# Soft-disc attention layer: paired norm-factor products, work moved from ScalarE to VectorE, and units of work in a new order

## The chip, the cores and the metric

The kernel runs on one core of a Trainium2 chip, in float32. The time is that of one execution in device microseconds (us). Engines go by the names of the profile: PE is TensorE's matmuls, PEld its weight loads, ACT is ScalarE, DVE is VectorE, POOL is GpSimd, SP is SyncE, which only issues transfers. Each engine works through its own list of instructions in the order in which the program gives them, and waits on semaphores where it needs another engine's result.

## The reference

The input is a batch of eight images of 32x32 tokens with 256 channels. Four layers follow one another, each `x = x + f(groupnorm(x))`. The change touches the last one, the soft-disc layer, whose `f` is, cut to what matters:

```python
qkv = silu(x @ w_qkv.T)
q, k, v = split(qkv, 3)                       # 8 heads of 32 channels
q = rope(rms_norm(q, w_qn)); k = rope(rms_norm(k, w_kn))   # norms per head
wp = silu(x @ w_wp.T + b_wp)                  # 16 columns: a width and a sharpness per head
width = sigmoid(wp[..., :8]) * max_dist + 0.5
sharp = sigmoid(wp[..., 8:]) * 9.5 + 0.5
scores = einsum(q, unfold(k)) / sqrt(32)      # 7x7 window around each token
soft_mask = sigmoid((width - rel_dist) * sharp)
attn = softmax(scores - (1 - soft_mask) * 10000)
out = einsum(attn, unfold(v))
return silu((rms_norm(out, w_on) + v) @ w_out.T)
```

The last norm runs over all 256 channels and has one weight per channel, `w_on`. The rope acts along the head axis's positions as the reference writes it; nothing of the change bears on it.

## The kernel before, in words

The kernel is a Python program that writes out the instructions of each engine. The soft-disc layer is `layer3` (L1950 on), with its attention in the class `DiscStream` (L1634 on).

**Tiling.** Channels lie on the 128 partitions, in two chunks of four heads; a chunk of an image is numbered J = 2b + c. Tokens are cut into 8 pairs of 8x8 blocks. A group is one pair of one chunk, so there are 8 x 2 x 8 = 128 groups, and the main loop takes one step n per group, 16 steps per image. Chunks are worked on well ahead of the step that uses them.

**A step** (the loop behind `start()`, at the end of `layer3`) writes, in this order: scores of n+3 on PE (16 matmuls of 32 rows, L1665); exponentials of n on ACT (`exps`, L1688, which also sum); the planned units due at n; logits of n+3 on DVE (L1678); the first half of `turn(n-2)`, PE transposes of the probabilities (`pt`, L1706) with a DVE copy to `pts` (L1711); `finish()`; `soft(n+5)`, the tanh of the disc on ACT (L2076); `divide(n)`, a DVE reciprocal (L1695) and a POOL product (L1696); the units due at n+0.5; the second half of the turn; `finish()`; `values(n-3)` on PE (`o`, L1722) with its DVE copies (L1730); and `masked(n+5)` on POOL (L2083). Probabilities live in a ring of nine tiles `e`.

**PSUM.** All PE outputs of the layer come from one ring of 8 banks (`st.ring(...)`), taken in the order written. A matmul into a bank waits until the last reader of the bank's earlier content is done.

**Units.** `Fillers` holds work with due times, in steps. `units(at)` emits what is due. A unit issues its PE part (and sometimes an ACT part) and may return a function, its rest; `finish()` calls all rests that are waiting. With n = 8J for a chunk and n = 16b for an image, the units and their due times are:

- `project(J, s, h)`: a projection of half an image (`qkv_ps`, L2015: PE, then a tanh on ACT, L2000; the rest on DVE, L2025/L2027, and for Q and K a POOL square, L2035). K at n-12 and n-11.5, Q at n-11 and n-10.5, V at n-7.5 and n-7.
- `roots(J, t)` at n-8: mean-square matmuls (`ms_ps`, L2095 for the heads, L2102 for the output norm of an earlier image) and, on ACT, a table load, Ln and Exp (L2109 to L2111) that give the factors `fac`; the next tanh loads the other table (L2076).
- `head_scale(J, s, h)`: one matmul of 32 rows that spreads a norm factor over the channels (`fac_ps`, L2117), and as its rest a DVE product with K or Q (L2121). At n-6, -5.5, -5 and -4.5.
- `in_strips` at n-6 copies values to padded strips on POOL; `vturn(J, u)`, five per chunk, transposes them on PE (`vt`, L1739) and copies them to `v` on ACT (L1744).
- `discs(b, u)` at n-10 and n-9.5: the width and sharpness (`wp_ps`, L2048), then in one rest a DVE add (L2055), an ACT tanh (L2060), a DVE product (L2061), an ACT tanh (L2062) and three small DVE operations from L2065.
- `normed(b, c)` at n-13.5 and n-13: the normalised input on ACT (L419).
- the tail of image b: `tail_sq` at n+19 and n+20 (POOL, L2145); four `tail_scale` at n+30, 30.5, 31, 31.5 (a 32-row matmul, L2150, DVE product L2154, POOL add L2155); `output` at n+33.5, 39, 39.5 and 41.5 (`out_ps`, L2163, an ACT tanh, a DVE product L2170, a POOL add L2172 and a store), with a `reload` three steps earlier.

In plain order of the engines' lists, units with the same due time stand in the order in which they were added. `First3.early` (L362 on) loads and prepares the constants, `won` and `spread` among them, long before the layer.

Of the kernel before, what the change touches and what calls it, by code (L numbers as in the profile page):

```python
# [32 lines left out]
def shape_constants():  # L33
    f = np.float32
    p = np.arange(P)
    k = {}

    k["k_id"] = np.stack(
        [np.eye(P), (p[:, None] // 8 == p[None] // 8) / 8.0], 1
    ).astype(f)  # L40


    same = (p[:, None] // 32 == p[None] // 32).astype(np.float64)
    k["k_hd"] = np.stack([np.eye(P) - same / 32, same / 32], 1).astype(f)
# [41 lines left out]
    one[:, 8] = 1.0  # L86
    k["k_sel3"] = np.concatenate(
        [(p[:, None] // 32 == np.arange(32)[None]) / 32.0, one / 256.0], 1
    ).astype(f)
    k["k_spread"] = (p[:, None] % 32 == p[None] // 32).astype(f)  # L90
    return {n: np.ascontiguousarray(v) for n, v in k.items()}


# [12 lines left out]
def layouts(inputs):  # L106
# [36 lines left out]
    a["l3_qkn"] = np.concatenate(  # L143
        [np.tile(i["L3_conv_w_" + n], 4) for n in ("qn", "kn")]
    )
    a["l3_on"] = i["L3_conv_w_on"].reshape(2, P)
    a.update(shape_constants())
    return {n: np.ascontiguousarray(v) for n, v in a.items()}

# [202 lines left out]
class First3(First):  # L352
# [8 lines left out]
    def early(self):  # L361
# [25 lines left out]
        def factors():  # L387
            won, spread = self.won, self.spread
            nc.vector.tensor_scalar(self.bwp, self.bwp, 0.5, None, ALU.mult)
            nc.gpsimd.tensor_scalar(self.wo, self.wo, 0.5, None, ALU.mult)  # L390
            nc.vector.tensor_mul(won[:, 0], won[:, 0], won[:, 1])
            nc.vector.scalar_tensor_tensor(
                spread[:, 0], won[:, 0], -(32.0**-0.5) / MASK_SCALE, spread[:, 0],
                ALU.mult, ALU.mult,
            )
            nc.vector.memset(won, 0.0)

        def weight():
            for h in range(2):
                nc.sync.dma_start(  # L400
                    self.won[32 * h + 8 : 32 * h + 9], a["l3_on"].unsqueeze(0)
                )

        return [loads, factors, weight]

# [1228 lines left out]
class DiscStream(Stream):  # L1634
# [7 lines left out]

    def __init__(self, K, wk, cp, pp, pairs, n_img, ebufs):
        super().__init__(K, wk, pp, pairs, n_img, ebufs)
        self.slots, self.s = 20, {}
        shape = [P, 4, 2 * self.PART]
        self.tiles = [cp.tile(shape, F32, name=f"e{i}") for i in range(ebufs)]

# [34 lines left out]

    def exps(self, n):
        mx, e = self.mx.pop(n), self.prob(n)
        self.su = self.wk.tile([P, 4], F32, name="su", bufs=4)
        for j in range(4):
            self.nc.scalar.activation(  # L1688
                e[:, j], e[:, j], AF.Exp, scale=-1.0, bias=mx[:, j : j + 1],
                accum_out=self.su[:, j : j + 1],  # L1690
            )

    def divide(self, n):
        e = self.prob(n)
        self.nc.vector.reciprocal(self.su, self.su)  # L1695
        self.nc.gpsimd.tensor_mul(e, e, self.su.unsqueeze(2).to_broadcast([P, 4, NWIN]))  # L1696

    def turn(self, n, i):

# [35 lines left out]
    def value_unit(self, strips, dst, u):  # L1735
        ps = self.ring("vt")
        for i in range(4):
# [3 lines left out]
                strips[:, col, 8 * r : 8 * r + 8].rearrange("p i j -> p (i j)"),  # L1741
                self.K.ident,
            )
        self.nc.scalar.copy(  # L1744
            dst[: self.PART, 4 * u : 4 * u + 4, :],
            ps[: self.PART, :].rearrange("p (s c) -> p s c", c=P),
        )
# [202 lines left out]
def layer3(tc, K, src, dst, n_img, a, first):  # L1950
    nc = tc.nc
    pairs = disc_pairs()
    with tc.tile_pool(name="l3c", bufs=1, reuse_waits="tile") as cp, tc.tile_pool(
# [14 lines left out]
        for i in range(3):  # L1968
            st.clear(i)
        K.ring = st.ring  # L1970
        bwp, sel, spread, won = first.bwp, first.sel, first.spread, first.won
        wo, win, eps = first.wo, first.win, first.eps

        gn = first.gn
# [66 lines left out]
        def discs(b, u):  # L2041
# [11 lines left out]
            def rest():  # L2053
# [2 lines left out]
                    d, ps.rearrange("p (t g) -> p t g", g=P)[:, :, 0:16],  # L2056
                    bwp.unsqueeze(1).to_broadcast([P, 4, 16]),
                )
                th = wk.tile([P, 4, 16], F32, name="dth")
                nc.scalar.activation(th, d, AF.Tanh)  # L2060
                nc.vector.scalar_tensor_tensor(d, th, 1.0, d, ALU.add, ALU.mult)  # L2061
                nc.scalar.activation(d, d, AF.Tanh, scale=0.5)  # L2062
                wd, sp = d[:, :, 0:8], d[:, :, 8:16]
                md = math.sqrt(2.0) * 3
                nc.vector.tensor_scalar(wd, wd, md / 2, md / 2 + 0.5, ALU.mult, ALU.add)  # L2065
# [45 lines left out]
            nc.scalar.activation(r[:n], r[:n], AF.Exp, scale=-0.5)  # L2111
            fac[J] = r

        def head_scale(J, s, h):
            g = slice(32 * (2 * s + h), 32 * (2 * s + h) + 32)
            ps = st.ring("fac_ps")
            nc.tensor.matmul(ps, spread[g, s], fac[J][g], start=True, stop=True)  # L2117

            def rest():
                d = dest(J, s, h)  # L2120
                nc.vector.tensor_mul(d, d, part(ps))  # L2121

            return rest

# [11 lines left out]
        def vturn(J, u):  # L2136
            b, c = divmod(J, 2)
            if u == 0:
                st.v[b, c] = wk.tile([P, st.slots, P], F32, name="v", bufs=2)
            st.value_unit(strips, st.v[b, c], u)  # L2140


        def tail_sq(b, c):
            sqs["o", c] = wk.tile([P, L], F32, name="sq", bufs=4)
            nc.gpsimd.tensor_mul(sqs["o", c], st.o[b, c], st.o[b, c])  # L2145

        def tail_scale(J, b, c, h):
            g, hs = slice(32 * h, 32 * h + 32), slice(h * HALF, (h + 1) * HALF)
            ps = st.ring("fac_ps")
            nc.tensor.matmul(ps, won[g, c], fac[J][g], start=True, stop=True)  # L2150

            def rest():
                d = st.o[b, c][:, hs]
                nc.vector.tensor_mul(d, d, ps)  # L2154
                nc.gpsimd.tensor_add(d, d, vT[b, c][:, hs])  # L2155

            return rest

# [26 lines left out]
        def plan_chunk(J):  # L2185
# [4 lines left out]
            for i in range(4):  # L2190
                s, h = 1 - i // 2, i % 2
                fill.add(n - 12 + i / 2, lambda s=s, h=h: project(J, s, h))
                fill.add(n - 6 + i / 2, lambda s=s, h=h: head_scale(J, s, h))
            fill.add(n - 7.5, lambda: project(J, 2, 0))
            fill.add(n - 7, lambda: project(J, 2, 1))
            fill.add(n - 6, lambda: in_strips(J))

        def plan_image(b):
            n = 16 * b
            if b:  # L2200
# [6 lines left out]
                fill.add(max(n - 21, -1), lambda: gn.mean(b, later))  # L2207
                fill.add(max(n - 19, 1), lambda: gn.root(b, later))
                for c in range(2):
                    fill.add(n - 13.5 + c / 2, lambda c=c: normed(b, c))  # L2210
                for u in range(2):
                    fill.add(n - 10 + u / 2, lambda u=u: discs(b, u))
            for c in range(2):
                fill.add(n + 19 + c, lambda c=c: tail_sq(b, c))
                for h in range(2):
                    fill.add(
                        n + 30 + c + h / 2,
                        lambda c=c, h=h: tail_scale(2 * b + 4, b, c, h),
                    )
            for i in range(4):  # L2220
                at = n + 32 + (1.5, 7, 7.5, 9.5)[i]
                fill.add(at - 3, lambda i=i: reload(b, i // 2, i % 2))
# [2 lines left out]
        for J in range(2 * n_img + 3):  # L2225
            b, c = divmod(J, 2)
            t = b - 2 if c == 0 and b >= 2 else None
            if J and (J < 2 * n_img or t is not None):
                fill.add(8 * J - 8, lambda J=J, t=t: roots(J, t))
            if J < 2 * n_img:  # L2230
                plan_chunk(J)
        for b in range(n_img):
            plan_image(b)
        for J in range(2 * n_img):
# [10 lines left out]
                    later.append(r)  # L2245

        def finish():
            while later:
                later.pop(0)()

        def start():

            units(-11)
            rest = [discs(0, 0), discs(0, 1), project(0, 1, 0)]
            rest[0]()
            rest[2]()
            r = project(0, 1, 1)
            rest[1]()
            r()
            soft(0)  # L2260
            for h in range(2):
                project(0, 0, h)()
# [4 lines left out]
            masked(0)  # L2267
            roots(0, None)
            in_strips(0)
            for i in range(4):  # L2270
                head_scale(0, 1 - i // 2, i % 2)()
            masked(1)
            for i in range(3, 9):
                st.clear(i)
# [4 lines left out]
        with tc.manual_schedule(engines={E.PE, E.Activation, E.DVE, E.Pool}):  # L2279
            start()  # L2280
            for n in range(-4, N + 3):
                if 0 <= n + 3 < N:
# [1 line left out]
                    if t is pairs[0]:  # L2284
                        st.o[b, c] = wk.tile([P, L], F32, name="oT", bufs=5)
                    st.scores(n + 3)
                if 0 <= n < N:
                    st.exps(n)
                units(n)
                if 0 <= n + 3 < N:  # L2290
                    st.logits(n + 3)
# [71 lines left out]
```

## Time and profile before

| what | value |
|---|---|
| time, median of 3 runs | 3330.99 us (3329.07 to 3332.86) |
| the profiled execution's own time | 3334.75 us |
| its span, first to last instruction | 3333.0 us |
| mean granted TensorE clock | 0.976 |
| busy over the span: PE, ACT, DVE, POOL | 3203.6, 2277.6, 2185.0, 1491.7 us |
| soft-disc layer | about 2540 us to the end |

Rows of instruction groups name the line, the engine, the tiles written and read, and the number of records; a 128x512 float32 matmul shows as two records. Rows of busy time by window give one stretch of the span each: its length, then the busy time and number of records of PE, PEld, DVE, ACT and POOL, the clock that TensorE was granted (1.00 is full), the share of the transfer engines and GB/s. Rows of the chain give start, length, engine, tile and line, from the work that ended last back to its releasers, printed in order of time.

### The profile page before, as it was taken

Reading aid. Unit: us, or ns where it says so; the run is one execution under the profiler, and the core shown is the slowest. Engines: PE = TensorE matmul, PEld = TensorE weight load, DVE = VectorE, ACT = ScalarE, POOL = GpSimd, SP = SyncE. Lnnn points to the kernel's source line nnn. Section 1 sums busy time; section 2 is a strip of 40 time slices with the busy share of each in tenths; the row PEclk is TensorE's granted clock in tenths of the full one; section 3 lists DMA queues with packets and bytes.
Section 4 is the critical chain, followed back from the end, with each engine's and each line's share of the span. In section 5 each row is a group of like instructions: output and inputs, shape, how many; then the busy total and the mean of one; then the engine's idle time right before and its main releaser. Section 6 shows DMA issues by size and latency. Waiting matters only on the chain. (4 is left out here: it accounts for less than half of the span.)

```text
span 3333.0 us, 77642 instructions
## 1 busy us (share of the span) xinstructions
PE 3203.6 (96%) x30792; PEld 1649.6 (49%) x30792; DVE 2185.0 (66%) x5570; ACT 2277.6 (68%) x5066; POOL 1491.7 (45%) x1073
## 2 busy tenths in 40 slices
PE   7999999999998999899999999999998999999997
PEld 3323323233232444667677766666664555555554
DVE  4776776777676667565555655666665667777775
ACT  3666666666676457755556547767676779888885
POOL 4233223323431011245444445344335658888777
PEclk9999999999999999999999999999998889999999
DMA  3000000000000666777787731111111001101001
GB/s 141 14 26 1 26 26 1 26 7 20 26 1 32 221 235 238 234 202 191 193 216 200 187 115 58 53 65 40 50 52 36 14 14 38 35 30 36 27 27 61
DMA packets 139183, 268.00 MB, mean 80 GB/s; under 512 B 9218, under 2 KB 77700, under 8 KB 130500
## 3 DMA queue, kind: packets, MB, share of 16 engines
q1 hardware_dynamic: 132436, 242.67, 24.3%
q10 hardware_dynamic: 6384, 20.37, 1.8%
q8 instruction: 243, 3.98, 0.5%
q14 instruction: 120, 0.98, 0.1%
HBM read 177.81 MB, written 85.20 MB: 79 GB/s over the span
## 5 line engine op out<-in xcount | busy, mean ns | idle before, releaser
L681 DVE TENSOR_TENSOR e<-s,ret 128x1024 f32<-128x1024 f32 x512 | 602.9, 1219 | 180.4 <-PE s L675 176.4
L685 ACT ACTIVATE ea<-e 128x1024 f32<-128x1024 f32 x512 | 535.1, 1055 | 267.8 <-DVE e L681 233.9
L675 PE MATMUL s<-qk,qk 32*128 32x512 f32 x2048 | 300.4, 640 | 2.4 <-POOL qk L567 1.7
L1564 POOL TENSOR_TENSOR e<-e,su 128x616 f32<-128x616 f32 (+2 forms) x128 | 157.3, 1229 | 269.8 <-DVE su L1563 240.2
L693 PE MATMUL sm<-ea,ones 128*32 128x512 f32 x2048 | 273.0, 604 | 2.0 <-DVE dn L701 2.0
L720 PE MATMUL num<-e,v 128*32 128x512 f32 x2048 | 266.6, 592 | 0.0
L1711 DVE COPY pts<-pt 112x512 f32<-112x512 f32 x256 | 175.9, 687 | 133.4 <-PE pt L1706 131.7
L2076 ACT ACTIVATE e<-win,disc 128x196 f32<-128x196 f32 x512 | 239.7, 544 | 0.3
L843 PE MATMUL up_ps<-x,wup 128*128 128x512 f32 x512 | 230.7, 605 | 3.2 <-POOL x L236 3.2
L1696 POOL TENSOR_TENSOR e<-e,su 128x784 f32<-128x784 f32 x128 | 191.3, 1495 | 82.7 <-DVE su L1695 53.9
L1688 ACT ACTIVATE e<-e,mx 128x196 f32<-128x196 f32 x512 | 228.0, 454 | 0.0
L2083 POOL TENSOR_TENSOR e<-e,win 128x784 f32<-128x784 f32 x128 | 201.7, 1576 | 37.8 <-issue 31.6
L1559 ACT ACTIVATE e<-e,mx 128x154 f32<-128x154 f32 (+2 forms) x512 | 212.3, 426 | 0.0
L1059 ACT ACTIVATE d<-d,cols 128x128 f32<-128x128 f32 x512 | 163.8, 392 | 67.9 <-POOL d L1050 67.8
L870 DVE SCALAR_TENSOR_TENSOR cv<-xm,par,cv 128x512 f32<-128x512 f32 x192 | 144.7, 754 | 85.5 <-ACT cv L865 80.9
L2015 PE MATMUL qkv_ps<-xq,w 128*128 128x512 f32 x384 | 191.4, 625 | 1.2 <-ACT fac L2110 1.2
L1255 POOL TENSOR_TENSOR decayed<-state,rb 128x520 f32<-128x520 f32 x48 | 50.8, 1058 | 304.7 <-PE sc L1188 112.5
L1796 PE MATMUL qkv_ps<-x,w 128*128 128x512 f32 x384 | 182.7, 613 | 1.6 <-POOL x L236 1.6
L1706 PEld LDWEIGHTS pt<-idg,e 128*112 128x112 f32 x1024 | 120.3, 139 | 120.5 <-issue 90.6
L675 PEld LDWEIGHTS s<-qk,qk 32*128 32x128 f32 x2048 | 85.3, 183 | 184.2 <-issue 120.4
L1706 PE MATMUL pt<-idg,e 128*112 128x128 f32 x1024 | 164.7, 287 | 8.4 <-DVE oT L1730 3.1
L1678 DVE CUSTOM_DVE_ANT_0 e<-s,e 128x196 f32<-128x196 f32 x512 | 153.7, 357 | 8.0 <-PE s L1665 4.2
(244 smaller groups left out, 6775.6 us busy)
## 6 DMA issues: line engine op xcount, KB each, us to landing
d<-l1rows SPq DMA_DIRECT2D x64, 512.0 KB
x<-x SPq DMA_DIRECT2D x25, 1024.0 KB
l1xm<-xm SPq DMA_DIRECT2D x16, 1024.0 KB
l1sz<-sz SPq DMA_DIRECT2D x16, 1024.0 KB
xv<-l1xm SPq DMA_DIRECT2D x32, 512.0 KB
l1xa<-xa SPq DMA_DIRECT2D x16, 1024.0 KB
xa<-l1xa SPq DMA_DIRECT2D x16, 1024.0 KB
rb<-l1rows SPq DMA_DIRECT2D x32, 512.0 KB
```

The lines of the kernel that those rows point to most:

```text
L675: nc.tensor.matmul(s[:, j % 2], qk[b, 1, c][g, kb * P : (kb + 1) * P], qk[b, 0, c][g, h * HALF : (h + 1) * HALF], start=True, stop=True,)
L681: nc.vector.tensor_mul(e[n, i], s, m)
L685: nc.scalar.activation(ea[n, i], e[n, i], AF.Abs)
L693: nc.tensor.matmul(acc["sm"][g, :], ones, ea[n, j // 2][:, j % 2, :], start=kb == 0, stop=kb == 7,)
L720: nc.tensor.matmul(acc["num"][g, :], v[b][:, kb, vc], e[n, j // 2][:, j % 2, :], start=kb == 0, stop=kb == 7,)
L843: nc.tensor.matmul(ps, wup[:, kc, m * P : (m + 1) * P], seg(s)[:, kc], start=kc == 0, stop=kc == 1,)
L1559: self.nc.scalar.activation(p[:, j], p[:, j], AF.Exp, scale=-1.0, bias=mx[:, j : j + 1], accum_out=su[:, j : j + 1],)
L1688: self.nc.scalar.activation(e[:, j], e[:, j], AF.Exp, scale=-1.0, bias=mx[:, j : j + 1], accum_out=self.su[:, j : j + 1],)
L1706: self.nc.tensor.transpose(ps[: self.PART, at : at + P], self.tile(n)[:, 2 * i + j, k * self.PART : (k + 1) * self.PART], self.K.ident,)
L2015: nc.tensor.matmul(ps, w[:, kc, o : o + P], xq[b][:, kc, h * HALF : (h + 1) * HALF], start=kc == 0, stop=kc == 1,)
L2076: nc.scalar.activation(e[:, j], win[:, 0], AF.Tanh, scale=disc[b][:, i, 8 + h : 9 + h], bias=disc[b][:, i, h : h + 1],)
L2083: nc.gpsimd.tensor_add(e, e, win[:, 1].unsqueeze(1).to_broadcast([P, 4, NWIN]))
```

## The change

Seven edits are made together, all in the soft-disc layer and the constants for it.

- `head_scale` takes both halves of K or of Q: two 32-row matmuls into two banks, one behind the other, on different rows of the array, and one rest with both DVE products. It is due at n-6 for K and n-5 for Q.
- The output norm's weight leaves the matmul. `won` now holds a selector of ones in row 8 of each 32 rows, and the weight as two columns; `tail_scale` makes one matmul per half image and multiplies both chunks with it on DVE, with the weight as a column scalar, each followed by its POOL add. Due at n+30 and n+31.
- The copy of the turned values goes from ACT to DVE, as the rest of `vturn`.
- The value projections are due at n-8.5 and n-8, and are added ahead of the roots of the next chunk, which stand at the same due time.
- `normed` is due at n-15 and n-14.5 (not before 2).
- `exps(n+1)` is written in step n, so that the sums are kept per group.
- `discs` returns its work in five links. `finish()` now calls each waiting function once, and what this returns waits for the next `finish()`.

```diff
             )
-            nc.vector.memset(won, 0.0)
 
         def weight():
-            for h in range(2):
-                nc.sync.dma_start(
-                    self.won[32 * h + 8 : 32 * h + 9], a["l3_on"].unsqueeze(0)
-                )
+
+            nc.sync.dma_start(self.won[:, 0], a["k_one8"])
+            nc.sync.dma_start(self.won[:, 1, 0:2], a["l3_on"])
...
     def exps(self, n):
         mx, e = self.mx.pop(n), self.prob(n)
-        self.su = self.wk.tile([P, 4], F32, name="su", bufs=4)
+        su = self.su[n] = self.wk.tile([P, 4], F32, name="su", bufs=4)
...
-        self.nc.scalar.copy(
+        return lambda: self.nc.vector.tensor_copy(
             dst[: self.PART, 4 * u : 4 * u + 4, :],
...
-                th = wk.tile([P, 4, 16], F32, name="dth")
-                nc.scalar.activation(th, d, AF.Tanh)
+                return silu
+
+            def silu():
+                th = wk.tile([P, 4, 16], F32, name="dth", bufs=2)
+                nc.scalar.activation(th, disc[b][:, 4 * u : 4 * u + 4, :], AF.Tanh)
+                return lambda: silu2(th)
+
+            def silu2(th):
+                d = disc[b][:, 4 * u : 4 * u + 4, :]
                 nc.vector.scalar_tensor_tensor(d, th, 1.0, d, ALU.add, ALU.mult)
+                return sigmoid
+
+            def sigmoid():
+                d = disc[b][:, 4 * u : 4 * u + 4, :]
                 nc.scalar.activation(d, d, AF.Tanh, scale=0.5)
+                return scales
+
+            def scales():
+                d = disc[b][:, 4 * u : 4 * u + 4, :]
                 wd, sp = d[:, :, 0:8], d[:, :, 8:16]
...
-        def head_scale(J, s, h):
-            g = slice(32 * (2 * s + h), 32 * (2 * s + h) + 32)
-            ps = st.ring("fac_ps")
-            nc.tensor.matmul(ps, spread[g, s], fac[J][g], start=True, stop=True)
+        def head_scale(J, s):
+
+            ps = [st.ring("fac_ps") for _ in range(2)]
+            for h in range(2):
+                g = slice(32 * (2 * s + h), 32 * (2 * s + h) + 32)
+                nc.tensor.matmul(ps[h], spread[g, s], fac[J][g], start=True, stop=True)
 
             def rest():
-                d = dest(J, s, h)
-                nc.vector.tensor_mul(d, d, part(ps))
+                for h in range(2):
+                    d = dest(J, s, h)
+                    nc.vector.tensor_mul(d, d, part(ps[h]))
...
-        def tail_scale(J, b, c, h):
+        def tail_scale(J, b, h):
+
             g, hs = slice(32 * h, 32 * h + 32), slice(h * HALF, (h + 1) * HALF)
             ps = st.ring("fac_ps")
-            nc.tensor.matmul(ps, won[g, c], fac[J][g], start=True, stop=True)
+            nc.tensor.matmul(ps, ones[g], fac[J][g], start=True, stop=True)
 
             def rest():
-                d = st.o[b, c][:, hs]
-                nc.vector.tensor_mul(d, d, ps)
-                nc.gpsimd.tensor_add(d, d, vT[b, c][:, hs])
+                for c in range(2):
+                    d = st.o[b, c][:, hs]
+                    nc.vector.scalar_tensor_tensor(
+                        d, d, on[:, c : c + 1], ps, ALU.mult, ALU.mult
+                    )
+                    nc.gpsimd.tensor_add(d, d, vT[b, c][:, hs])
...
-                fill.add(n - 6 + i / 2, lambda s=s, h=h: head_scale(J, s, h))
-            fill.add(n - 7.5, lambda: project(J, 2, 0))
-            fill.add(n - 7, lambda: project(J, 2, 1))
+            for s in range(2):
+                fill.add(n - 5 - s, lambda s=s: head_scale(J, s))
+            fill.add(n - 8.5, lambda: project(J, 2, 0))
+            fill.add(n - 8, lambda: project(J, 2, 1))
...
-                    fill.add(n - 13.5 + c / 2, lambda c=c: normed(b, c))
+                    fill.add(max(n - 15, 2) + c / 2, lambda c=c: normed(b, c))
...
+            if J < 2 * n_img:
+                plan_chunk(J)
             if J and (J < 2 * n_img or t is not None):
                 fill.add(8 * J - 8, lambda J=J, t=t: roots(J, t))
-            if J < 2 * n_img:
-                plan_chunk(J)
...
         def finish():
-            while later:
-                later.pop(0)()
+
+            due = later[:]
+            later[:] = [r for r in [f() for f in due] if callable(r)]
...
-                if 0 <= n < N:
-                    st.exps(n)
+                if 0 <= n + 1 < N:
+                    st.exps(n + 1)
```

More of the change, by code (lines that the diff above doesn't have):

```diff
@@ L90, in shape_constants @@
     k["k_spread"] = (p[:, None] % 32 == p[None] // 32).astype(f)
+    k["k_one8"] = np.tile(p[:, None] % 32 == 8, (1, P)).astype(f)
     return {n: np.ascontiguousarray(v) for n, v in k.items()}
@@ L145, in layouts @@
     )
-    a["l3_on"] = i["L3_conv_w_on"].reshape(2, P)
+    a["l3_on"] = _cols(i["L3_conv_w_on"])
     a.update(shape_constants())
@@ L1644, in __init__ @@
         super().__init__(K, wk, pp, pairs, n_img, ebufs)
-        self.slots, self.s = 20, {}
+        self.slots, self.s, self.su = 20, {}, {}
         shape = [P, 4, 2 * self.PART]
@@ L1689, in exps @@
                 e[:, j], e[:, j], AF.Exp, scale=-1.0, bias=mx[:, j : j + 1],
-                accum_out=self.su[:, j : j + 1],
+                accum_out=su[:, j : j + 1],
             )
     def divide(self, n):
-        e = self.prob(n)
-        self.nc.vector.reciprocal(self.su, self.su)
-        self.nc.gpsimd.tensor_mul(e, e, self.su.unsqueeze(2).to_broadcast([P, 4, NWIN]))
+        e, su = self.prob(n), self.su.pop(n)
+        self.nc.vector.reciprocal(su, su)
+        self.nc.gpsimd.tensor_mul(e, e, su.unsqueeze(2).to_broadcast([P, 4, NWIN]))
     def turn(self, n, i):
@@ L1970, in layer3 @@
         K.ring = st.ring
-        bwp, sel, spread, won = first.bwp, first.sel, first.spread, first.won
+        bwp, sel, spread = first.bwp, first.sel, first.spread
+        ones, on = first.won[:, 0], first.won[:, 1, 0:2]
         wo, win, eps = first.wo, first.win, first.eps
@@ L2139, in vturn @@
                 st.v[b, c] = wk.tile([P, st.slots, P], F32, name="v", bufs=2)
-            st.value_unit(strips, st.v[b, c], u)
+            return st.value_unit(strips, st.v[b, c], u)
         def tail_sq(b, c):
@@ L2214, in plan_image @@
                 fill.add(n + 19 + c, lambda c=c: tail_sq(b, c))
[L2215 to L2219, printed above, removed]
+                fill.add(n + 30 + c, lambda c=c: tail_scale(2 * b + 4, b, c))
             for i in range(4):
@@ L2247, in finish, with all_of @@
         def finish():
-            while later:
-                later.pop(0)()
+            due = later[:]
+            later[:] = [r for r in [f() for f in due] if callable(r)]
+        def all_of(*rests):
+            while rests:
+                rests = [r for r in [f() for f in rests] if callable(r)]
         def start():
@@ L2254, in start @@
             rest = [discs(0, 0), discs(0, 1), project(0, 1, 0)]
[L2255 to L2259, printed above, removed]
+            all_of(rest[0], rest[2])
+            all_of(rest[1], project(0, 1, 1))
             soft(0)
@@ L2269, in start @@
             in_strips(0)
-            for i in range(4):
-                head_scale(0, 1 - i // 2, i % 2)()
+            for s in (1, 0):
+                head_scale(0, s)()
             masked(1)
```

## The prediction

> **What bounds the kernel now.** I read the page first. TensorE (PE) is busy for 96% of the whole run, so the stage that the change touches, the soft-disc layer from about 2540 us on, has to be read on its own.
>
> ```profile
> span 3333.0 us, 77642 instructions
> PE 3203.6 (96%) x30792; PEld 1649.6 (49%) x30792; DVE 2185.0 (66%) x5570; ACT 2277.6 (68%) x5066; POOL 1491.7 (45%) x1073
> PEclk9999999999999999999999999999998889999999
> ```
>
> Second view: busy time by window. An image of this layer takes 91.15 us (2922.91 to 3014.06 to 3105.24, end of the scores of like steps). In both whole images PE works for 88.5 of 91 us, ACT for 80.75, POOL for 73.9, DVE for 69.2. The rows at PEclk 0.50 to 0.52 show PE full at half its clock.
>
> ```profile
> core 0: us, PE busy (x) PEld busy (x) DVE busy (x) ACT busy (x) POOL busy (x), PEclk, DMA share, GB/s
> 2574.00:2594.00 20.00, 18.95 (x99) 8.49 (x100) 12.04 (x52) 15.71 (x49) 12.72 (x10) 0.50 0.17 53
> 2731.00:2744.00 13.00, 13.00 (x101) 6.28 (x100) 9.07 (x37) 6.67 (x24) 8.62 (x7) 0.51 0.00 1
> 2923.00:3014.00 91.00, 88.48 (x961) 49.58 (x956) 69.18 (x268) 80.75 (x233) 73.87 (x56) 1.00 0.12 36
> 3014.00:3105.00 91.00, 88.47 (x964) 49.47 (x956) 69.17 (x268) 80.75 (x233) 73.83 (x56) 1.00 0.12 36
> ```
>
> Third view: the chain that ended last, inside one image (start, us, what). Outside two stretches it runs on PE. The first exception is 16 us on ACT, 2946.15 to 2962.09, around the roots: value copies, disc tanhs, exponentials, table load, Ln, Exp, table load, then a projection's tanh and a value copy, after which PE's first norm-factor product of the next chunk may start. The second is the disc, where DVE and ACT take turns from 2985.0 to 2996.66.
>
> ```profile
> 2925.13 1.05 PE fac_ps L2117 x2
> ...
> 2939.25 1.05 PE fac_ps L2150 x2
> ...
> 2946.15 0.59 ACT v L1744
> ...
> 2950.78 1.28 ACT L2109
> 2952.07 0.70 ACT fac L2110
> 2952.79 0.63 ACT fac L2111
> 2953.43 1.28 ACT L2076
> ...
> 2962.09 1.12 PE fac_ps L2117 x2
> ...
> 2985.01 0.69 DVE pts L1711
> 2987.00 1.54 ACT e L2076 x4
> 2989.42 1.46 DVE disc L2061
> ```
>
> So two numbers matter: what leaves PE, and what becomes of the ACT stretch at each of the 15 roots of later chunks.
>
> **The change part by part.**
>
> *Paired norm-factor products.* A 32-row product of two records holds PE for 1.05 us; a chunk has four, one behind another. The change issues them two by two on different row groups. No row here shows two of these together; the nearest is the score products, also 32 rows on different groups: 16 of them, 0.35 us mean, take 0.52 us together in the chain (0.68 where only 11 records are in the piece), not 5.6. I take full overlap: 2 x 1.05 = 2.1 us less per chunk, 15 chunks, 31.5 us. Bounds: 0 (no overlap) and 31.5. In steps 2 and 3 of each half image PE is the bound (step 3 takes 4.36 us, the sum of PE's pieces s 0.52, fac 1.05, pt 0.58, fac 1.05, pt 0.58, o 0.58), so there it comes off the path. By the Trainium skill, "TensorE: Matmul & The Clock Gate", Part 3 (packing small matmuls), products on distinct row groups start within 4 ns of each other; its figure, worked out for a pair, is an estimate of the same 1.05 us saved per pair, and no run here has shown it for this shape.
>
> *Output norm.* Four products become two per image, since the weight goes into a DVE instruction with a column scalar. 2 x 1.05 = 2.1 us of PE at steps 14 and 15, for the seven images whose tail lies beside another image: 14.7 us. DVE's four 0.677 us products become four scalar-tensor-tensor of the same size; the output's (0.683 us) are the nearest, so nothing. POOL's four 1.27 us adds stay. The eighth tail is in the closing stretch, where POOL adds and output transfers make the end: nothing, within 0.5.
>
> *Turned values.* Ten copies of 0.573 us per image leave ACT (5.7 us) and go to DVE, where the same shape (pts, 112x512) takes 0.689 us: DVE goes from 69.2 to 76 of 91 us. In the ACT stretch three of them go (1.64 us), the last being what PE waited for at 2962.09. But the copy is now queued on DVE behind logits and output, so a bank of the eight in the ring can come free later. Bounds: a gain of 1.64 and a loss of 0.69 at each roots.
>
> *Values ahead of roots.* The two value projections (1.72 to 1.91 us each) now stand one step earlier, so that the second is ahead of the mean-square products (1.07 + 1.70 us in the tail's chunk) and not behind the roots. Ln can then start up to 1.9 us later, and its 1.28 + 0.69 + 0.63 + 1.28 = 3.9 us of ACT with it, as can everything behind it there. The two tanhs of 0.58 us move from behind the roots to ahead, which changes only the order. The first falls into steps 7 and 15, already the fullest. Bounds per roots: 0 and +1.9 us.
>
> *Normalised input 1.5 steps earlier.* Two ACT instructions of 1.24 us per image move to step 1, into the ACT stretch of every second roots: 0 to 2.5 us there, 1.2 us per roots at most on the mean.
>
> *Exponentials a step ahead.* DVE's reciprocal and POOL's division no longer wait for the same step's exponentials. POOL's division waited 36.3 us on the reciprocal between 2700 and 3200 us; POOL is not the bound, so I price it at nothing (cover: PE). If PE stops being the cover, it is a gain of at most 36.3 / 5.5 = 6.6 us per image. A tile of the ring is held a step longer; the ring has nine and the turn follows three steps later, so no wait is added.
>
> *Disc in links.* The disc chain's waits of ACT on DVE (12.1 + 4.2 us in those 500 us) and of DVE on ACT (6.9) were inside a stretch where PE still worked 11.79 of 13 us. Gain at most 1.2 us per image; priced at nothing, as the output's tanhs are late next.
>
> *Moves on the queues.* SP loses two one-row loads and gains two small ones long before use; the reorderings near the end change no input that is late. Nothing. At the start of the layer, where the DVE chain leads (2554 to 2562 us), five copies come onto DVE at up to 0.69 us: bounds 0 and +2.8 us, I take +1.4.
>
> Sum. PE gives 31.5 + 14.7 = 46.2 us. Given back at each roots: from the bounds -1.64 to +0.69, 0 to +1.9 and 0 to +1.2, i.e. -1.6 to +3.8; I take +1.5, nearer the upper end, because the chain shows ACT without a pause there, with ACT busy 13.92 of 14 us in each such window and PE 12.7 to 13.3. 15 x 1.5 = 22.5 us. So -46.2 + 22.5 + 1.4 = -22.3. The profiled execution took 3334.75 us, its span being 3333.0 and 1.75 outside it: 3334.75 - 22.3 = 3312.45. It is 3.76 us above the median of the three runs, 3330.99, so 3308.7, or 3309 us.
>
> **The clock.** PE is granted half its clock for 20.5 us from 2573.9, and for 13.65 us each from 2631.9, 2679.7, 2730.9 and 3147.3. Inside the spell of 2731 a step of PE pieces took 8.40 us (2734.05 to 2742.45) against 4.36 at full clock, so a spell costs 48% of its length, 6.6 us for 13.65. All follow an ACT stretch and start with norm-factor products. I leave them as they are in the sum. The rows: from 2727.6 to 2731.0 PE was busy 3.06 of 3.40 us, and the clock fell to 0.52 after it. The same page, Part 1, has half the clock come after an idle window of about 3.4 us; by that rule this spell would not exist and the paired products could not matter to it. The row differs, and the row decides: a busy PE is not enough where the work is 32 rows deep.
>
> **The rivals.**
>
> *Full gain.* Nothing is given back and four spells of 13.65 us go, since pairs halve the thin work: -46.2 - 26.4 + 1.4, 3260 us on the scale of the median. For: PE is 97% busy in whole images, and ACT loses 5.7 us each. Against: the ACT stretch. With half of either, 3285.
>
> *ACT at the roots decides (slower).* The value projection in front delays Ln; the output's tanh and the two bank releases behind it stay as late, and PE waits for its second product. Price per roots: 1.9 for the projection, 1.24 for the normalised input, 0.58 for a tanh, 0.68 for the output's DVE product in front of the copy, 4.4 us; 15 x 4.4 = 66, so -46.2 + 66 + 1.4 = +21, 3352 us. It turns slower from 46.2 / 15 = 3.1 us per roots on. For: ACT's 13.92 of 14 us. Against: three value copies leave ACT just there.
>
> *DVE binds at steps 14 and 15.* Four value copies (2.8 us) join the tail's products on DVE, so that the 14.7 us of the output norm are not gained: 3309 + 14.7 = 3324 us. Against: DVE works 15.0 of 22 us in that window.
>
> *Pairs do not overlap.* Then 31.5 us are missing: -14.7 + 22.5 + 1.4 = +9, 3340 us. Against: the score rows.
>
> **How the numbers follow.** Likeliest as summed, own range 3297 to 3320 us: 0.37. Full or half gain with fewer spells, 3262 to 3297: 0.25. DVE at the tail: 0.10, a third of it faster by over 0.2%. ACT at the roots: 0.22, two thirds slower. Pairs without overlap: 0.06. A measurement of this kernel can tell about 0.2%, 6.7 us: same is 3324.3 to 3337.7. Faster 0.37 + 0.25 + 0.03 = 0.65; same 0.07 of DVE and some 0.04 of ACT, 0.11; slower 0.18 + 0.06, 0.24. For 8 in 10 I leave out the fullest gains and the worst roots: 3270 to 3345.
>
> **What the profile would show.** Right: a pair of fac products in one piece of about 1.1 us; steps 3 and 11 near 3.3 us; no value copies on ACT, ten per image on DVE near 0.6 us; an image of 85 to 89 us. Wrong: a PE wait of over 3.1 us at each roots, on the table load, the tanh of the output or the value copy; half-clock spells that are more or longer than now; a pair of 2.1 us.

## The result and the profile after

The changed kernel takes 3343.65 us (median of five runs, 3339.31 to 3347.27) against 3330.99 us: a ratio of 1.0037, 95% interval 1.0023 to 1.0052. It is slower by some 12 us where 22 us less were forecast. Its profiled execution has a span of 3340.2 us, 7.2 us over that of before.

The page of the changed kernel, the lines that answer to those shown of before:

```profile
span 3340.2 us, 77644 instructions
PE 3197.3 (96%) x30760; PEld 1662.3 (50%) x30760; DVE 2220.1 (66%) x5649; ACT 2238.9 (67%) x4986; POOL 1491.8 (45%) x1073
PEclk9999999999999999999999999999998999899888
```

ACT's busy time fell by 38.7 us and DVE's rose by 35.1, the way that the 80 moved copies work. PE's fell by only 6.3 us, and its clock is now below full in more slices. Dividing the span by the ends of like steps shows where the time went:

| stretch | before | after | difference |
|---|---|---|---|
| start of the span to step -2 | 2557.7 | 2556.8 | -0.8 |
| steps -2 to 32 (two images and a little more) | 208.0 | 180.3 | -27.7 |
| steps 32 to 112 (five images) | 462.5 | 494.4 | +31.9 |
| step 112 to the end | 104.8 | 108.7 | +3.9 |

So the change gains 28 us while the layer is young and has no output and almost no tail to do, and loses more in the later images: 98.9 us for the image of steps 64 to 80 against 91.2. In busy time by window (length, then PE, PEld, DVE, ACT, POOL, then the granted clock), the changed kernel's image and two places in it:

```profile
2936.70:3035.60 98.90, 93.15 (x968) 53.34 (x952) 73.47 (x278) 76.44 (x223) 74.09 (x56) 0.90 0.11 33
2946.20:2949.60 3.40, 1.16 (x10) 0.29 (x2) 0.00 (x0) 3.40 (x11) 2.42 (x2) 1.00 0.02 5
2949.60:2953.00 3.40, 1.62 (x2) 0.50 (x2) 2.36 (x11) 3.40 (x11) 1.59 (x2) 0.52 0.00 0
3000.70:3014.40 13.70, 13.70 (x108) 7.63 (x107) 11.07 (x45) 8.30 (x30) 8.96 (x7) 0.51 0.12 38
```

Two things show. From 2946.2 on, PE and DVE wait while ACT is busy without a pause; in the next window PE has half its clock. And there is a second half-clock spell of 13.7 us in the other half of the image. The half-clock spells that begin between 2750 and 3245 us add up to 109.2 us in the changed kernel and to 17.1 in the kernel before; between 2540 and 2750 us it is the other way round, 30.7 against 68.3.

Which wait is it? PE's instructions in order of time (start, length, line, tiles; in brackets the idle time ahead of one and what ended it), in the next image of the changed kernel:

```profile
3035.80 1.98 PE L2015 MATMUL qkv_ps<-xq,w 128*128 128x512 f32 x4
3037.72 1.07 PE L2110 MATMUL ms_ps<-sq,sel 128*32 128x512 f32 x8
...
3041.31 1.88 PE L2185 MATMUL out_ps<-oT,wo 128*128 128x512 f32 x4
...
3045.10 1.12 PE L2134 MATMUL fac_ps<-fac,spread 32*128 32x512 f32 x2
3050.25 2.07 PE L2134 MATMUL fac_ps<-fac,spread 32*128 32x512 f32 x2 [4.03 <-DVE th L2192]
```

The second product of K's pair takes the bank that the first output projection used. It waits 4.03 us until DVE's product has read that bank, which waits for the output's tanh on ACT. The chain of work says why ACT is late; it starts with the mean-square products and runs through ACT without a pause:

```profile
3037.79 1.00 PE ms_ps L2110 x8
...
3039.81 0.68 ACT fac L2125
...
3041.16 1.28 ACT L2091
...
3044.34 1.77 ACT e L1687 x8
3046.10 1.13 ACT xq L418
3047.24 1.77 ACT e L2091 x4
3049.00 0.48 ACT th L2000
...
3049.51 0.70 DVE th L2192
...
3050.25 2.07 PE fac_ps L2134 x2
```

In the kernel before, PE did the same mean-square products, and between them and the norm-factor products it had two value projections of 1.9 and 2.0 us to do:

```profile
2949.65 1.07 PE L2095 MATMUL ms_ps<-sq,sel 128*32 128x512 f32 x8
...
2951.13 1.88 PE L2015 MATMUL qkv_ps<-xq,w 128*128 128x512 f32 x4
...
2954.49 1.98 PE L2015 MATMUL qkv_ps<-xq,w 128*128 128x512 f32 x4
...
2958.01 1.95 PE L2163 MATMUL out_ps<-oT,wo 128*128 128x512 f32 x4 [1.10 <-ACT e L1688]
...
2962.09 1.12 PE L2117 MATMUL fac_ps<-fac,spread 32*128 32x512 f32 x2 [0.16 <-ACT v L1744]
```

In the changed kernel both stand ahead of the mean-square products. ACT's stretch is as long as it was: from Ln to the output's tanh 9.0 us before, 9.2 us after.

The second spell, at step 10, has no such wait ahead of it. K's pair waits 0.77 us there, for a DVE copy; ACT had finished the norm factors 7 us earlier (the Exp ends at 2992.81 us). Of the 3.40 us ahead of the spell PE was busy 2.58, most of it in products 32 rows deep. First the window, then PE's instructions in it:

```profile
2997.60:3001.00 3.40, 2.58 (x42) 1.14 (x31) 3.15 (x10) 3.40 (x12) 1.79 (x3) 0.99 0.02 5
2997.88 1.45 PE L1664 MATMUL s<-kp,qT 32*64 32x196 f32 x16
3000.10 2.91 PE L2134 MATMUL fac_ps<-fac,spread 32*128 32x512 f32 x4 [0.77 <-DVE pts L1710]
```

### The profile page after: what moved, and what is told of

It is laid out like the page before. It is cut to its first block, busy times and chain, and to the rows that moved or that the text cites. A ratio compares the mean times of both kernels' runs of the same rounds, so it can differ in the third digit from the quotient of the medians.

```text
span 3340.2 us, 77644 instructions
## 1 busy us (share of the span) xinstructions
PE 3197.3 (96%) x30760; PEld 1662.3 (50%) x30760; DVE 2220.1 (66%) x5649; ACT 2238.9 (67%) x4986; POOL 1491.8 (45%) x1073
## 4 chain that ended last, share of the span: by engine, by line
PE 76%; ACT 8%; POOL 5%; DVE 5%; issue 4%; DMA 1%; ACTq 0%; POOLq 0%; SPq 0%; DVEq 0%
PE s L674 8%; PE sm L692 7%; PE num L719 6%; PE qkv_ps L1795 5%; PE up_ps L842 5%; PE qkv_ps L2015 5%; PE pt L1705 3%; PE pt L1577 3%; PE qk_ps L549 3%; PE dn_ps L1322 2%; PE o_ps L602 2%; PE pr_ps L1855 2%; PE o L1596 2%; PE s L1537 2%; PE v_ps L533 2%
## 5 line engine op out<-in xcount | busy, mean ns | idle before, releaser
L1705 PEld LDWEIGHTS pt<-idg,e 128*112 128x112 f32 x1024 | 130.5, 148 | 90.9 <-issue 51.5
```

Of the source, the lines that this page charges most:

```text
L1705: self.nc.tensor.transpose(ps[: self.PART, at : at + P], self.tile(n)[:, 2 * i + j, k * self.PART : (k + 1) * self.PART], self.K.ident,)
```

## The experiments

The theory (A) was that the value projections had been the cover of PE's wait for the roots, and that the wait and the half clock that follows it make the loss. The rivals were the normalised input and the exponentials in front of the output's tanh (B), the bank alone, and a clock that falls because the paired products are thin.

**The values behind the roots again**, all else as changed.

```diff
-            fill.add(n - 8.5, lambda: project(J, 2, 0))
-            fill.add(n - 8, lambda: project(J, 2, 1))
+            fill.add(n - 7.5, lambda: project(J, 2, 0))
+            fill.add(n - 7, lambda: project(J, 2, 1))
```

> The changed kernel with one part undone: the value projections are due at n-7.5 and n-7 again, behind the roots. In the changed kernel PE stands still for 4.0 us in step 2 of a later image, waiting at the second norm-factor product for the output's DVE product and the tanh on ACT before it, and half-clock spells of 6.8 us (step 2) and 13.7 us (step 10) follow in each image. Theory A (lost cover): the two projections, 3.6 us of PE work, used to fill just that wait; with them back behind the roots the wait falls to under 1 us, the spells of the later images go, an image takes 86 to 90 us in place of 98.9, and the time is 3285 to 3310 us. Rival B (the output's tanh is late because the normalised input, 1.24 us, and the exponentials stand ahead of it): the wait stays above 2.5 us and the spells stay, time within 8 us of the changed kernel's 3343. Rival C (the clock falls because the paired products thin the work, wait or no wait): the wait goes but the spells stay, time 3320 to 3335 us.

Measured: 3281.83 us, ratio to before 0.9844 (0.9819 to 0.9869). One line of due times takes off 62 us from the changed kernel. In its PE instructions the projections stand behind the mean-square products, and the wait is a tenth:

```profile
2906.55 1.07 PE L2110 MATMUL ms_ps<-sq,sel 128*32 128x512 f32 x8
...
2908.03 1.88 PE L2015 MATMUL qkv_ps<-xq,w 128*128 128x512 f32 x4
...
2911.39 1.98 PE L2015 MATMUL qkv_ps<-xq,w 128*128 128x512 f32 x4
...
2917.56 1.12 PE L2134 MATMUL fac_ps<-fac,spread 32*128 32x512 f32 x2
2919.10 1.51 PE L2134 MATMUL fac_ps<-fac,spread 32*128 32x512 f32 x2 [0.42 <-DVE th L2192]
```

From step 32 to step 112 an image takes 88.0 to 92.9 us. The spells did not all go: two images keep one of 10.2 us, and half clock after 2540 us falls from 163.7 to 64.6 us. But for these spells it is as theory A expected, and 3 us better than its range.

**The values ahead of the roots, alone, in the kernel before**: the same due times the other way, with chunks planned ahead of roots as in the change.

```diff
-            fill.add(n - 7.5, lambda: project(J, 2, 0))
-            fill.add(n - 7, lambda: project(J, 2, 1))
+            fill.add(n - 8.5, lambda: project(J, 2, 0))
+            fill.add(n - 8, lambda: project(J, 2, 1))
```

> The kernel before with one part of the change alone: the value projections due at n-8.5 and n-8, ahead of the roots. Putting them back in the changed kernel took 62 us off its median (3343.65 to 3281.83). Theory A (lost cover): the projections cover the wait for the roots also here, so taking them away costs here too; PE has 4.2 us more work per chunk here (unpaired products), so less of it shows: +20 to +60 us, 3350 to 3395 us. Rival B (only together with the other parts, which bring PE to the roots earlier, does it hurt): within 10 us of before, 3320 to 3345 us.

Measured: 3399.27 us, ratio 1.0192 (1.0174 to 1.0209), +66 us, a little beyond the range of A; the rival falls. Here every half image has a half-clock spell of 13.7 or 17.1 us, 259.3 us in all, and an image takes 105.8 us:

```profile
2971.50:3077.30 105.80, 102.03 (x968) 54.91 (x956) 69.03 (x268) 81.32 (x233) 74.22 (x55) 0.85 0.10 31
```

PE is busy for 102.0 us of this image, against 88.5 of 91 us before with the same work. So of the 14.7 us more, 13.4 are PE working at a lower clock and only 1.3 are waiting: here the projections had covered hardly any wait, and had kept the clock up. This one part costs 62 to 66 us on either side, and the other six together gain about 50.

**The normalised input late again**, all else as changed.

```diff
-                    fill.add(max(n - 15, 2) + c / 2, lambda c=c: normed(b, c))
+                    fill.add(n - 13.5 + c / 2, lambda c=c: normed(b, c))
```

> The changed kernel with one part undone: the normalised input is due at n-13.5 and n-13 again. Theory A (lost cover): the wait in step 2 shrinks by the 1.24 us of one ACT instruction, from 4.0 to about 2.8 us; the spells stay, time 3330 to 3345 us. Rival B (the normalised input is what made the output's tanh late): the wait and the spell of step 2 go, those of step 10 stay, time 3310 to 3325 us.

Measured: 3330.59 us, ratio 0.9989 (0.9979 to 1.0000). The wait is 2.90 us, as A says: one ACT instruction shorter, not gone; the spells stay (156.7 us). Moving this input into the stretch had cost some 13 us all the same.

**Useless wide products in the wait.**

```diff
             ps = [st.ring("fac_ps") for _ in range(2)]
+            for _ in range(3 if s else 0):
+                nc.tensor.matmul(ps[0], w[:, 0, 0:P], w[:, 0, 0:HALF], start=True, stop=True)
```

> The changed kernel with three useless 128-row products of 512 columns (0.86 us each at full clock) written into the first bank of the pair, ahead of K's norm-factor products; the pair overwrites them. They fill the PE wait of step 2 with wide work and put 2.6 us into step 10. If the half-clock spells are set by thin or missing PE work and cost 48% of their length, the spells of both steps go: 20.5 us of half clock per image times 0.48 = 9.8 us gained, less up to 2.6 us at step 10: an image of 90 to 93 us in place of 98.9, time 3300 to 3320 us. If the spells are a mere sign of waits (the clock costs nothing that ACT did not cost already), the time is 3340 us or more.

Measured: 3319.13 us, ratio 0.9956 (0.9938 to 0.9973). More work on PE made the kernel 24.5 us faster. Half clock after 2540 us falls from 163.7 to 57.8 us; the image of steps 64 to 80 takes 95.6 us, not the 90 to 93 expected, since a wait of 1.25 us is left and the useless products, at step 10 above all, cost their own time. So the clock is a cost of its own. Its share can be read from PE's busy time. The changed kernel's image, shown above, takes 98.9 us with PE busy for 93.15; an image without a spell, in the last row of the next experiment, takes 87.9 us with PE busy for 85.81, for nearly the same work. Of the 11.0 us between them about 7.3 are slower work and 3.7 are waiting. That makes the 20.5 us of half clock cost some 36% of their length, not the 48% that one step had given.

**The first output later.**

```diff
-                at = n + 32 + (1.5, 7, 7.5, 9.5)[i]
+                at = n + 32 + (4.5, 7, 7.5, 9.5)[i]
```

> The changed kernel with the first of four output projections of an image due three steps later (n+36.5 in place of n+33.5), behind the norm-factor products, so that their second bank no longer waits for the output's tanh. Theory A (lost cover): PE then waits for ACT in another place, at most the tanh and the DVE product (0.6 + 0.7 us) come off, and the wait of 4.0 us becomes one of 1 to 3 us; time 3320 to 3340 us. Rival B (it is the bank alone): the wait goes, the spell of step 2 goes and that of step 10 stays, time 3300 to 3320 us.

Measured: 3313.47 us, ratio 0.9934 (0.9914 to 0.9954). The rival's range holds it: the spell of step 2 went, that of step 10 stayed (13.7 us at 2890, 2985). So the 4.0 us of step 2 went through the bank, and A was wrong to expect another wait there. The spell of step 10 needs the values behind the roots, or the wide products; the fourth output, which stands ahead of K's pair there, was not moved. With both edits:

> The variant with the values behind the roots (3281.83 us) and the first output projection three steps later, behind the norm-factor products. That variant still waits 0.42 us for the output's DVE product at the second product of step 2, with a spell of 10.2 us at half clock there in two of its images. If the output's bank is what is left: the spells go, 2 x 4.9 us, 3268 to 3278 us. If ACT's stretch is too long in any order: within 6 us, 3276 to 3288 us.

Measured: 3277.11 us, ratio 0.9828 (0.9813 to 0.9842), the fastest median of all, 4.7 us under the variant without it, which is inside the overlap of the two intervals; the ranges of both readings hold it. The 0.42 us of waiting and the two spells of 10.2 us are gone, but spells of 13.7 and 6.8 us stand in other steps. Against the run before, the values' move costs 36 us once the output is later, not 62. An image with no spell, or one of 3.4 us, takes 87.8 to 88.0 us:

```profile
2910.70:2998.60 87.90, 85.81 (x962) 49.88 (x952) 72.68 (x278) 75.85 (x222) 74.53 (x56) 1.00 0.13 38
```

**The copies of turned values on ACT**, with the values behind the roots.

```diff
-        return lambda: self.nc.vector.tensor_copy(
+        self.nc.scalar.copy(
```

> The variant with the values behind the roots (3281.83 us) and the copies of turned values back on ACT. If the ACT stretch at the roots is what sets the pace, 5.7 us of ACT work per image come back, 1.64 us of it in the stretch: +1.6 us at each of 15 roots, +25 us or more with the spells, 3300 to 3320 us. If PE alone sets it: within 6 us, 3276 to 3288 us. My bounds in the prediction were a gain of 1.64 us and a loss of 0.69 us per roots for this part.

Measured: 3284.78 us, ratio 0.9862 (0.9837 to 0.9887): no difference that these runs can tell. Inside, it is two effects. Steps 15 and 0 take 4.04 and 4.24 us with the copies on ACT and 4.74 and 5.16 on DVE, so DVE does hold up those steps; the step with the first output takes 10.36 us in place of 6.17, so ACT's stretch takes it back.

**Single norm-factor products**, with the values behind the roots: the old `head_scale` and its four due times.

```diff
-            for s in range(2):
-                fill.add(n - 5 - s, lambda s=s: head_scale(J, s))
+                fill.add(n - 6 + i / 2, lambda s=s, h=h: head_scale(J, s, h))
```

> The variant with the values behind the roots (3281.83 us) and the norm-factor products single again, at n-6, -5.5, -5 and -4.5. My prediction priced the pairs at 2.1 us per chunk, 31.5 us: then 3305 to 3320 us. If what the pairs save is waited for elsewhere: 3278 to 3300 us. With more spells at half clock, since the thin work is longer: above 3320 us.

Measured: 3319.78 us, ratio 0.9954 (0.9936 to 0.9972), with a wide spread (3299.6 to 3329.92). The pairs are worth 38 us. Half clock rises from 64.6 to 129.7 us; at 36% of its length, as above, that is an estimate of 23 of the 38 us, and the pairs' own time would be the rest. No run separates the two.

**The exponentials in their own step**, with the values behind the roots.

```diff
-                if 0 <= n + 1 < N:
-                    st.exps(n + 1)
+                if 0 <= n < N:
+                    st.exps(n)
```

> The variant with the values behind the roots (3281.83 us) and the exponentials written in their own step again. I priced this part at nothing because PE covers it, with 6.6 us per image as the most it could bring. PE as cover: within 6 us, 3276 to 3288 us. If the division's wait for the reciprocal now stands on the path: 8 images of 1 to 6.6 us, 3290 to 3335 us.

Measured: 3278.94 us, ratio 0.9827 (0.9805 to 0.9849). The part does nothing that can be measured, as with PE for cover. In the changed kernel itself, where these exponentials stand ahead of the output's tanh, they were not moved alone.

**The disc as one rest**, with the values behind the roots.

```diff
-                    fill.add(n - 10 + u / 2, lambda u=u: discs(b, u))
+                    fill.add(n - 10 + u / 2, lambda u=u: (lambda r: lambda: all_of(r))(discs(b, u)))
```

> The variant with the values behind the roots (3281.83 us) and the disc chain written as one rest again. I priced the links at nothing, at most 1.2 us per image, since PE worked 11.79 of 13 us in that stretch. PE as cover: within 10 us, 3276 to 3292 us. If the turns of ACT and DVE hold up exponentials and copies that PE waits for now that it has less work: 2 to 4 us per image, 3295 to 3315 us.

Measured: 3296.95 us, ratio 0.9889 (0.9869 to 0.9909). The links are worth 15 us. In the step after the disc, PE stands still for the turned copy that DVE has not come to, which it does not with the links:

```profile
2960.00 0.62 PE L1705 MATMUL pt<-idg,e 128*112 128x128 f32 x4 [0.99 <-DVE v L1743]
```

That step takes 7.66 us against 6.48, and steps -2 to 32 take 179.2 against 171.1.

**Two attempts at a better version**: values behind the roots, copies on ACT, first output later; and the same with the normalised input late again.

> The variant with the values behind the roots, the copies of turned values on ACT, and the first output three steps later. With the copies on ACT, steps 15 and 0 of an image took 4.04 + 4.24 us against 4.74 + 5.16 with them on DVE, so DVE sets those steps; but the step with the first output took 10.36 us, behind the output's tanh. If both readings hold, an image takes 85 to 87 us (87.8 with the copies on DVE and the output later, 3277.11 us), time 3262 to 3274 us. If ACT's stretch takes back what DVE gives: 3274 to 3285 us.

> As the run with the copies on ACT and the first output later, and the normalised input at n-13.5 and n-13 again, out of the ACT stretch at the roots. If ACT's stretch at the roots is still what PE waits for: 1.2 us less in each of 8 images, 6 to 12 us under that run. If it is covered: within 5 us of it.

Measured: 3291.7 us (ratio 0.9874, 0.9853 to 0.9895) and 3282.62 us (0.9851, 0.9824 to 0.9878). Neither beats 3277.11, and the first lies above both of its ranges. The two gains do not add: with the copies on ACT, the step before the norm-factor products takes 8.2 us even without the output, and three spells of 13.7 us are left. Taking the normalised input out of the stretch wins 9 us there by the medians (the two intervals overlap) and takes these spells away, in line with the first of its two readings.

## Why the prediction was wrong

**Values ahead of roots** is the step that failed, and it is also what "given back at each roots" was made of. I had bounded it by 0 and +1.9 us per roots, as a delay of Ln. Ln did come later relative to PE, but what counts is the other side of the move: the two projections, 3.6 to 3.9 us of PE work, had stood between PE and the result it needed. Taken away from there, they left a wait of 4.0 us at every second roots and, ahead of the norm-factor products, work too thin to keep the clock. My rows showed it: in the kernel before, PE was busy 12.74 of 14 us in that stretch, while the chain ran on ACT. I read this as ACT being the bound and did not ask which PE work filled it. Undone, the part gives 62 us, 4.1 us per roots, against 1.5 in the sum and a bound of 3.8 for all that happens there; the point that I had worked out, 3.1 us per roots, was passed. Of the rivals, "ACT at the roots decides" named the place, the very wait (PE's second product, for the output's tanh and the bank behind it) and, with 4.4 us per roots, nearly the size. The size is partly luck: it was made of delays alone, and by PE's busy time only a third of the loss is waiting.

**The clock** is the second error, and by PE's busy time the larger one: I left the spells as they were in the sum, a term of nothing, where slower work is about two thirds of the loss in the changed kernel and nearly all of it with the values moved alone. In the stretch without cover PE did 1.16 us of work in 3.40 us, and had half the clock in the next window: these spells follow the wait that I had priced at 1.5 us. Those of step 10 follow 2.58 us of narrow work in 3.40, with hardly a wait. The Trainium skill, "TensorE: Matmul & The Clock Gate", Part 1, puts half the clock behind an idle window of about 3.4 us. I had set that rule aside because one row, 3.06 of 3.40 us busy, differs from it. The window of 1.16 us is nearer to the rule, though not idle either; that of 2.58 us differs from it as my row did. That a busy PE is not enough where the work is 32 rows deep was my own reading, and I did not carry it into the sum, where the change takes two wide products away from just that place.

**Paired products.** The overlap was right for a pair whose banks are both free: four records, a pair, make one piece.

```profile
3055.91 1.06 PE fac_ps L2134 x4
```

That is 1.06 us for a pair, as for one product before, so this row shows the 1.05 us per pair that I had estimated with the Trainium skill, "TensorE: Matmul & The Clock Gate", Part 3. But not every pair is such a pair. Of the 30 pairs of the later chunks, the two products start together (within 0.02 us) in 14 in the changed kernel and in 5 with the values behind the roots. In the changed kernel the others are mostly K's, whose second product waits for its bank. In the variant the second product of 18 pairs starts some 0.6 us late:

```profile
3015.20 1.72 PE L2134 MATMUL fac_ps<-fac,spread 32*128 32x512 f32 x4
```

The step of Q's pair, forecast near 3.3 us, takes 3.18 us with full overlap, 3.78 with the late start and 4.36 with single products. So the 31.5 us were too much for PE's own time: about 0.6 us per pair, 18 us for 30, is the estimate from that step. The part is worth 38 us there all the same, since the clock adds to it, in the early images too, where I had not looked for it.

**The rest of the sum.** The other six parts together gain about 49 us by the medians, against the 46.2 us that I had for PE alone; this nearness is chance, since neither the pairs nor the clock came out as priced. By the two spans 36.9 us come before step 32, where half clock falls from 68.3 to 13.7 us (20 to 26 us at 36 to 48%), and 15.3 us in the five images after, where I had expected 6.3 each. **Turned values**: between the bounds, as measured. **DVE at steps 14 and 15**: the rival was right about the place; 1.6 us per image are lost there. **Normalised input**: 1.2 us per roots at most was the bound; undone in the changed kernel it gives about 13 us, 0.9 per roots. **Exponentials**: nothing, as priced. **Disc in links**: priced at nothing because PE worked 11.79 of 13 us; it is worth 15 us. The row shows a turned copy, which now stands on DVE, waiting behind the disc; that PE's cover is thinner because PE has less work is argued, not tried. **The layer's start**: the span to step -2 came out 0.8 us shorter, where I took +1.4 in bounds of 0 to 2.8; but it holds three layers that the change leaves alone, and it runs from 2549 to 2559 us in the profiles of these runs, so it cannot judge the term. **The closing stretch**, where I expected no change, is 3.9 us longer from step 112 on; with the values behind the roots it is 1.6 us longer than before, so the larger part of it belongs to the values as well.

What I said would show the forecast wrong is what the profile shows: a wait of over 3.1 us on the output's tanh, though only at every second roots, and more half-clock spells.

## What to carry to other kernels

Before moving work ahead of a latency, ask what it covers where it stands, a wait or the clock: ahead of the roots the same instructions cost 62 us more than behind them. A share of "PE 97% busy" does not say that less PE work is a gain; look at what stands between an engine's request to another and its use of the answer. And where the trace shows a granted clock that falls after thin or missing matmul work, price the spell along with the wait, and count narrow work with the idle time.

## What was not expected of the hardware

Three useless 128-row products per chunk made the kernel 24.5 us faster (3343.65 to 3319.13 us), since they kept the granted clock up: 57.8 us at half clock in place of 163.7. The clock does not need an idle PE to fall: it fell to 0.52 after a window in which PE was busy 3.06 of 3.40 us, with much of it 32 rows deep, and in the changed kernel after one of 2.58 of 3.40. Making that work denser by pairs halved the time at half clock (129.7 to 64.6 us).
